# Mixing's weights moved from between the loads of x to behind all of them

## The chip, the cores and the metric

The kernel runs on one core of a Trainium2 chip. The metric is device time in microseconds (us): the time of one execution of the whole program. A kernel's time is the median of its runs; one further execution is taken with the hardware profiler, and every duration below comes from that one.

## The reference, cut to what matters

The input x has 16 images of 64 channels of 128 x 128, in float32. A Hartley layer (a spectral convolution) takes its 20 x 20 lowest modes, mixes the channels of each mode with a weight, transforms back, blurs, and masks. An AFNO block with group norms and a mixture of experts follows.

```python
def dht_2d(x):
    return fftn(x, axes=(2, 3)).real - fftn(flip(x, axis=(2, 3)), axes=(2, 3)).imag
def _neg_k(a):
    return roll(flip(a, axis=(-2, -1)), shift=(1, 1), axis=(-2, -1))
def compl_mul2d(x1, x2):                       # x2: w1, (64, 64, 20, 20)
    x1n, x2n = _neg_k(x1), _neg_k(x2)
    e = lambda a, b: einsum('bixy,ioxy->boxy', a, b)
    return 0.5 * (e(x1, x2) - e(x1n, x2n) + e(x1, x2n) + e(x1n, x2))
x_ht = dht_2d(x)
out_ht[:, :, :20, :20] = compl_mul2d(x_ht[:, :, :20, :20], w1)
y = dht_2d(out_ht) / (H * W)
y = gaussian_smoothing_4d(y)                   # blur over batch, channels, rows, columns
return y * mask                                # |fftfreq(W)| <= 0.25
# then: group norm, AFNO on 32 x 32 modes, residual, group norm, and per image
# a 1x1 feature layer, 2 shared experts, a gate, the best 4 of 16 experts, residual
```

What matters for the change is `_neg_k`: each mode k is mixed with w[k] and also with w[-k], the weight of the mode with both indices negated modulo 20. So a tile with w[k] in its lower half and w[-k] in its upper half is wanted, and the second is w with its inner axis reversed.

## The kernel before

The work runs in a chain of stages: the first ones lie in the first 470 us or so, and the last, the loop over images, takes the rest.

**The x loop** (from L240 on). For each image b of 16 the channels go in eight groups of eight. Each group is one load `xt` of 512 KB on SP's queue (L245, ten buffers, so that SP runs up to ten tiles ahead), 16 matmuls with `fwd1` (L250, the transform along one axis), and one ScalarE copy to `t1` (L253). After the second group of an image comes `along_columns` (L205 to L237) for the image before: 80 matmuls with `fwd2` (L212), a ScalarE copy `pn` (L215), six VectorE additions into `xm` (L219 to L222), and the blur over the batch: VectorE adds `xm`, times a factor, into `x2` for up to nine images (L231, L233). When an image of `x2` has its last term, ScalarE makes its second half (L236, L237). TensorE, ScalarE and VectorE each go through this in the program's order; a DMA is issued when the instructions before it on its queue's engine are through and the waits of its own are met.

**The weights of mixing** sit in `wk` [128, 11, 20, 64]: for k1 = 0 to 10 the lower 64 partitions hold w[k1] as it is in memory, the upper 64 hold w[-k1] with its second index reversed, too. DRAM has them by k1 in pieces of 320 KB. Before the change, at the end of image b (b = 0 to 10) SP issues two loads: the lower half straight to `wk` (L264), the upper half to one staging tile `wn` (L265). At the end of the next image ScalarE copies `wn` to the upper half of `wk`, the first row as it is (L261, 64x64) and the other 19 in reverse order (L262, 64x1216).

**Constants.** Behind the x loop SP issues, by the helper at L172, the loads `blurc`, `dev`, `mean`, `gn1`, `ident`, `sel`, `w1`, `vec`, `spec` (3.2 MB on 100 partitions) and `exw`. Their memory is on the right side, which the x loop used till then, so the first of them waits for the x loop's end.

**Mixing** (L283 on). For k1 = 0 to 10: 20 matmuls, weights from `wk`, data from `x2` (L294), into `psm` (two buffers); then evacuations into `om`, two on ScalarE and one on VectorE beside them or in turn (ScalarE L298, L301, L302; VectorE L299, L303).

**What follows**: the blur over channels (L312; evacuated into `ot` by ScalarE L319 and VectorE L321), the first group norm's statistics (matmuls L397 with `mean`, L406 with `dev`, squares on ScalarE L408, and VectorE's small work L429 to L471), then the AFNO stage per image (L548 with `spec`), and the loop over images (from L826's experts to the store). SP loads the tables of the later stages, `v2` first, between mixing and the statistics; ScalarE copies `v2` to `v2a` and `v2b` (L509 to L514) in two groups of six.

Of the kernel before, what the change touches and what calls it, by code (L numbers as in the profile page):

```python
# [19 lines left out]
K = 20  # L20
# [139 lines left out]
def hartley_afno_moe_kernel(ctx: ExitStack, tc: tile.TileContext, a: dict, out: bass.AP):  # L160
# [6 lines left out]
    def load(pool, name, shape, eng=None):  # L167
        t = pool.tile(shape, F32, name=name + "_sb", tag=name)
        src = a[name]
        if len(shape) == 3 and len(src.shape) == 2:  # L170
            src = src.rearrange("p (a b) -> p a b", b=shape[2])
        (eng or nc.sync).dma_start(t, src)  # L172
        return t
# [13 lines left out]
    with tc.tile_pool(name="modes", bufs=1) as mp:  # L187

        x2 = mp.tile([P, 2, NB, NM], F32, name="x2")
        wk = mp.tile([P, K // 2 + 1, K, C], F32, name="wk")
        gb = blur_matrix(NB)
        with tc.tile_pool(name="f_x", bufs=10) as xp, tc.tile_pool(name="f_t", bufs=2) as tp, \
                tc.tile_pool(name="f_c", bufs=1) as fc, \
                tc.tile_pool(name="f_p1", bufs=4, space=PSUM) as pp1, \
                tc.tile_pool(name="f_p2", bufs=2, space=PSUM) as pp2:
            fwd1 = load(fc, "fwd1", [P, W1], nc.gpsimd)
            fwd2 = None

            wn = fc.tile([P, K, C], F32, name="wn")
            seen = set()

            def along_columns(b, t1):


                ps = pp2.tile([P, K // 2, W1], F32, name="ps2")
                for m in range(K // 2):
                    for t in range(2):
                        for h in range(2):  # L210
                            j = 2 * (2 * m + h) + t
                            nc.tensor.matmul(ps[h * C:(h + 1) * C, m, :], lhsT=t1[:, j, :],  # L212
                                             rhs=fwd2[:, j, :], start=(t == 0), stop=(t == 1))
                pn = tp.tile([P, K // 2, K], F32, name="pn")
                nc.scalar.copy(pn, ps[:, :, K:2 * K])  # L215
                xm = tp.tile([P, K, K], F32, name="xm")
                for half, op in ((0, ALU.add), (1, ALU.subtract)):
                    to = xm[half * C:(half + 1) * C]
                    nc.vector.tensor_tensor(to[:, 0:1], ps[0:C, 0:1, 0:K], pn[0:C, 0:1], op)  # L219
                    nc.vector.tensor_tensor(to[:, 2:K:2], ps[0:C, 1:, 0:K],  # L220
                                            pn[0:C, K // 2 - 1:0:-1], op)
                    nc.vector.tensor_tensor(to[:, 1:K:2], ps[C:P, :, 0:K],  # L222
                                            pn[C:P, ::-1], op)
                xf = xm.rearrange("p a b -> p (a b)")
                for bo in range(NB):
                    g = float(gb[bo, b])
                    if g == 0.0:
                        continue
                    to = x2[:, 0, bo, :]
                    if bo in seen:  # L230
                        nc.vector.scalar_tensor_tensor(to, xf, g, to, ALU.mult, ALU.add)  # L231
                    else:
                        nc.vector.tensor_scalar(to, xf, g, None, ALU.mult)  # L233
                        seen.add(bo)
                    if not gb[bo, b + 1:].any():
                        nc.scalar.mul(x2[0:C, 1, bo], x2[C:P, 0, bo], -1.0)  # L236
                        nc.scalar.copy(x2[C:P, 1, bo], x2[0:C, 0, bo])  # L237

            behind = None
            for b in range(NB):  # L240

                t1 = tp.tile([P, 2 * K, C], F32, name="t1")
                for c0 in range(0, C, 8):
                    xt = xp.tile([P, 8, N], F32, name="xt")
                    nc.sync.dma_start(xt, a["x"][b, :, c0:c0 + 8])  # L245
                    ps = pp1.tile([P, 8, W1], F32, name="ps1")
                    for i in range(8):
                        for h in range(2):
                            cols = slice(h * 64, (h + 1) * 64)
                            nc.tensor.matmul(ps[cols, i, :], lhsT=xt[:, i, cols],  # L250
                                             rhs=fwd1, start=True, stop=True)
                    src = ps[:, :, 0:2 * K].rearrange("p c j -> p j c")
                    nc.scalar.copy(t1[:, :, c0:c0 + 8], src)  # L253
                    if c0 == 8 and behind:
                        along_columns(*behind)
                behind = (b, t1)
                fwd2 = fwd2 or load(fc, "fwd2", [P, 2 * K, W1])

                if 0 < b <= K // 2 + 1:
                    k = b - 1  # L260
                    nc.scalar.copy(wk[C:P, k, 0], wn[C:P, 0])  # L261
                    nc.scalar.copy(wk[C:P, k, 1:K], wn[C:P, K - 1:0:-1])  # L262
                if b <= K // 2:
                    nc.sync.dma_start(wk[0:C, b], a["w"][b])  # L264
                    nc.sync.dma_start(wn[C:P], a["w"][(-b) % K])  # L265
            along_columns(*behind)

        sc = on_modes.enter_context(tc.tile_pool(name="s_c", bufs=1, side="right"))
        blurc = load(sc, "blurc", [P, C])
        dev = load(sc, "dev", [CH, 4, NM])  # L270
        mean = load(sc, "mean", [CH, 4, C])
        gn1 = load(sc, "gn1", [P, 2, C])
        ident = load(sc, "ident", [P, C])
        sel = load(sc, "sel", [CH, 5, 32])
        w1 = load(sc, "w1", [P, 2, P])
        vec = load(const, "vec", [P, V_N])
        spec = load(sc, "spec", [CH, 4, 2 * MD * MD])
        exw = load(sc, "exw", [P, C, NE])

        with tc.tile_pool(name="m_o", bufs=1) as op, \  # L280
                tc.tile_pool(name="m_p", bufs=2, space=PSUM) as pp, \
                tc.tile_pool(name="m_p2", bufs=4, space=PSUM) as pp2:


            om = [op.tile([P, NB, NM // 2], F32, name=f"om{h}") for h in range(2)]
            lok, upk = (t[h * C:(h + 1) * C].rearrange("o b (k2 k1) -> o k1 k2 b", k1=K)
                        for h, t in enumerate(om))
            for k1 in range(K // 2 + 1):

                ps = pp.tile([P, K // 2, 2, NB, 2], F32, name="psm")  # L290
                for m in range(K // 2):
                    k = k1 * K + 2 * m
                    for h in range(2):
                        nc.tensor.matmul(ps[h * C:(h + 1) * C, m].rearrange("p a b q -> p (a b q)"),  # L294
                                         lhsT=wk[:, k1, 2 * m + h, :], rhs=x2[:, :, :, k:k + 2],
                                         start=True, stop=True)
                lo, up = ps[0:C, :, :, :, 0], ps[C:P, :, :, :, 1]
                nc.scalar.copy(lok[:, k1], lo[:, :, 0])  # L298
                nc.vector.tensor_copy(upk[:, k1], up[:, :, 0])  # L299
                if k1 % (K // 2):  # L300
                    nc.scalar.copy(lok[:, K - k1, 0:1], lo[:, 0:1, 1])  # L301
                    nc.scalar.copy(lok[:, K - k1, K // 2 - 1:0:-1], lo[:, 1:, 1])  # L302
                    nc.vector.tensor_copy(upk[:, K - k1, ::-1], up[:, :, 1])  # L303


            for b0 in range(0, NB, 8):
                for cc in range(2):
                    pq = [pp2.tile([CH, 8, C], F32, name="pst") for h in range(2)]
                    for i in range(8):
                        for h, (m0, m1) in ((0, (0, C)), (1, (C, CH)), (1, (0, C)), (0, (C, CH))):  # L310
                            g = slice(h * C, (h + 1) * C)
                            nc.tensor.matmul(pq[h][m0:m1, i, :],  # L312
                                             lhsT=om[h][g, b0 + i, cc * CH + m0:cc * CH + m1],
                                             rhs=blurc[g], start=True, stop=True)
                    for h in range(2):
                        dst = ot[:, 2 * h + cc, b0 * C:(b0 + 8) * C]
                        src = pq[h].rearrange("p b c -> p (b c)")
                        if h:
                            nc.scalar.copy(dst, src)  # L319
                        else:  # L320
                            nc.vector.tensor_copy(dst, src)  # L321


    s3 = ctx.enter_context(ExitStack())
# [635 lines left out]
```

## Time and profile before

| | |
|---|---|
| median of 3 runs | 1856.39 us |
| lowest and highest run | 1854.67 and 1856.52 us |
| the profiled execution: its time | 1848.89 us |
| the profiled execution: its span | 1846.9 us |
| mean granted TensorE clock | 0.976 |
| PE (TensorE matmul) busy | 1701.5 us, 92% |
| ACT (ScalarE) busy | 1378.3 us, 75% |
| DVE (VectorE) busy | 1270.7 us, 69% |
| POOL (GpSimd) busy | 120.9 us, 7% |
| DMA | 181.00 MB, 98 GB/s over the span |

PE, ACT, DVE, POOL and SP are the engines (SP only issues DMAs); PEld is TensorE's weight load, which runs beside the matmuls. L294 is line 294 of the kernel. The profile page cuts the span into 40 slices of 46.2 us and prints the busy share of each engine in tenths, for PEclk the TensorE clock that was granted. A row of windows has, for a stretch of time, the busy time and count of each engine's instructions, the granted clock, the share of the 16 DMA engines that was in use, and GB/s. A row of waits has the engine's instruction, what released it, the idle time, the number of times and the longest. "issue" stands for idle time in which the engine waited for nothing that the profile shows. A row of the timeline has the start, the duration, the engine, the line, what is written and read, and in brackets the idle time ahead and what ended it.

### The profile page before, as it was taken

The numbers are of one execution on the slowest core, as the hardware profiler recorded it, in microseconds if no ns is written. First come the engines' busy times: TensorE is split into PE (matmuls) and PEld (weight loads), VectorE is DVE, ScalarE is ACT, GpSimd is POOL, SyncE is SP. The second block draws the span as 40 slices with busy tenths as digits, with TensorE's granted clock in tenths as the row PEclk, the third lists the DMA queues.
The fourth block names the chain that finished last, engine by engine and source line by source line (L and its number), as shares of the span: only waits on it lengthen the run. The fifth ranks groups of instructions, "written<-read, shape, count | busy, mean of one in ns | idle before, by whom it ended". The sixth has DMA issues, their size and how long they took to land. (4 is left out here: it accounts for less than half of the span.)

```text
span 1846.9 us, 55817 instructions
## 1 busy us (share of the span) xinstructions
PE 1701.5 (92%) x24644; PEld 940.8 (51%) x24644; DVE 1270.7 (69%) x1774; ACT 1378.3 (75%) x1690; POOL 120.9 (7%) x140
## 2 busy tenths in 40 slices
PE   6777769999899999999999999999999999999996
PEld 6776765333645455454545555454545455554521
DVE  1233432322249788797979797797979797887988
ACT  2343343112488998989898999989898999989897
POOL 0000002003010101010110101010100101010110
PEclk8899988999999999999999999999999999999998
DMA  9999841115212222222332222322232322222023
GB/s 337 319 322 326 285 145 48 69 52 145 47 25 70 48 81 57 84 36 82 57 72 58 59 82 36 99 41 81 37 86 53 71 72 46 72 57 71 27 72 92
DMA packets 136129, 181.00 MB, mean 98 GB/s; under 512 B 94201, under 2 KB 95414, under 8 KB 135658
## 3 DMA queue, kind: packets, MB, share of 16 engines
q1 hardware_dynamic: 132192, 171.73, 33.1%
q0 software_dynamic: 3696, 5.71, 1.2%
q8 instruction: 193, 3.16, 0.7%
q14 instruction: 48, 0.39, 0.1%
HBM read 98.29 MB, written 79.11 MB: 96 GB/s over the span
## 5 line engine op out<-in xcount | busy, mean ns | idle before, releaser
L834 DVE SCALAR_TENSOR_TENSOR h<-g,wt,h 128x1024 f32<-128x1024 f32 x512 | 620.9, 1275 | 85.2 <-ACT g L831 85.2
L831 ACT ACTIVATE g<-pe,wl 128x1024 f32<-128x1024 f32 x512 | 539.4, 1131 | 8.9 <-PE pe L826 8.2
L826 PE MATMUL pe<-f,wl 64*64 64x512 f32 x4096 | 494.7, 600 | 1.3 <-issue 0.4
L834 DVE SCALAR_TENSOR_TENSOR h<-g,h 128x1024 f32<-128x1024 f32 x256 | 301.6, 1220 | 56.1 <-ACT g L831 56.1
L831 ACT ACTIVATE g<-pe,vec_sb 128x1024 f32<-128x1024 f32 x256 | 278.7, 1135 | 20.6 <-PE pe L826 20.4
L669 PEld LDWEIGHTS pe<-inv_sb,u 107*128 107x128 f32 x2048 | 234.4, 192 | 64.9 <-ACT g L831 33.2
L826 PEld LDWEIGHTS pe<-f,wl 64*64 64x64 f32 x4096 | 135.6, 132 | 237.3 <-ACT g L831 98.6
L826 PE MATMUL pe<-f,shw 64*64 64x512 f32 x2048 | 252.9, 604 | 0.0
L669 PE MATMUL pe<-inv_sb,u 107*128 107x128 f32 x2048 | 248.8, 279 | 3.2 <-ACT g L831 1.9
L677 ACT ACTIVATE h<-pe,gs 128x1024 f32<-128x1024 f32 x128 | 142.6, 1115 | 73.2 <-PE pe L669 57.3
L250 PE MATMUL ps<-fwd_sb,xt 128*64 128x64 f32 x4096 | 141.5, 232 | 51.0 <-issue 43.1
L681 DVE BATCH_NORM_STATS2 stats<-h 128x6 f32<-128x512 f32 x256 | 160.1, 679 | 25.9 <-ACT h L677 25.8
L250 PEld LDWEIGHTS ps<-fwd_sb,xt 128*64 128x64 f32 x4096 | 135.9, 147 | 54.7 <-issue 46.6
L647 PE MATMUL pe<-inv_sb,bm 64*64 64x128 f32 (+1 forms) x4096 | 144.8, 275 | 1.2 <-issue 1.2
L736 ACT ACTIVATE f<-pe,fb 128x1024 f32<-128x1024 f32 x128 | 144.3, 1137 | 2.2 <-PE pe L732 2.2
L647 PEld LDWEIGHTS pe<-inv_sb,bm 64*64 64x64 f32 (+1 forms) x4096 | 118.5, 124 | 48.1 <-ACT f L736 24.3
L253 ACT COPY t<-ps 128x320 f32<-128x320 f32 x128 | 54.0, 427 | 114.4 <-PE ps L250 114.0
L732 PE MATMUL pe<-h,fs 64*64 64x512 f32 x1024 | 133.9, 611 | 1.6 <-DVE n L709 1.6
L652 ACT COPY u<-pe 105x1024 f32<-105x1024 f32 x128 | 127.4, 1043 | 3.9 <-PE pe L647 2.9
L219 DVE TENSOR_TENSOR xm<-ps,pn 64x20 f32<-64x20 f32 x32 | 5.5, 171 | 172.5 <-ACT pn L215 172.2
L548 PE MATMUL psx<-spec_sb,ot 100*64 100x512 f32 x512 | 115.6, 594 | 0.0
L806 POOL DMA_INDIRECT wl<-exd,ati x64 | 66.9, 1045 | 697.4 <-ACT g L831 605.4
(164 smaller groups left out, 1163.5 us busy)
## 6 DMA issues: line engine op xcount, KB each, us to landing
xt<-in_x_dram SPq DMA_DIRECT2D x128, 512.0 KB
out_dram<-h SPq DMA_DIRECT2D x256, 256.0 KB
o1d<-o SPq DMA_DIRECT2D x16, 512.0 KB
s<-o1d SPq DMA_DIRECT2D x16, 512.0 KB
bm<-od SPq DMA_DIRECT2D x96, 50.0 KB
wk<-in_w_dram SPq DMA_DIRECT2D x11, 320.0 KB
wn<-in_w_dram SPq DMA_DIRECT2D x11, 320.0 KB
spec_sb<-in_spec_dram SPq DMA_DIRECT2D x1, 3200.0 KB
```

The source lines that it names most:

```text
L250: nc.tensor.matmul(ps[cols, i, :], lhsT=xt[:, i, cols], rhs=fwd1, start=True, stop=True)
L548: nc.tensor.matmul(ps[ri * C:(ri + 1) * C], lhsT=ot[:, kc, b * C:(b + 1) * C], rhs=spec[:, kc, ri * 1024 + n * 512:ri * 1024 + (n + 1) * 512],
L647: nc.tensor.matmul(ps[cs, h, i, :], lhsT=bm[rs, 4 * q + i, cs], rhs=inv1[rs, part], start=True, stop=True)
L652: nc.scalar.copy(dst.rearrange("p h s n -> p n h s"), ps[0:KC].rearrange("p h s n -> p n h s"))
L669: nc.tensor.matmul(ps[:, r // 4, r % 4 * N:(r % 4 + 1) * N], lhsT=u[0:KU, 2 * row:2 * row + 2, :].rearrange("p h c -> p (h c)"), rhs=inv2, ...
L677: nc.scalar.activation(h, ps, AF.Identity, bias=gs1[:, 1, box["b"]:box["b"] + 1])
L681: nc.vector.bn_stats(box["stats"][:, 2 * t + p, :], h[:, p])
L732: nc.tensor.matmul(ps[p * C:(p + 1) * C, half], lhsT=box["fs"][rows_], rhs=box["h"][t][rows_, p], start=True, stop=True)
L736: nc.scalar.activation(f, ps, AF.Gelu, bias=box["fb"], accum_out=box["sums"][:, t:t + 1])
L826: nc.tensor.matmul(ps[half * C:(half + 1) * C, p], lhsT=w[rows_], rhs=f[rows_, half], start=True, stop=True)
L831: nc.scalar.activation(g, ps, AF.Gelu, bias=bias)
L834: nc.vector.scalar_tensor_tensor(h, g, share(), h, ALU.mult, ALU.add)
```

## The change

All loads and copies of mixing's weights leave the loop over images. The eleven lower halves are loaded behind the last x tile, ahead of the last `along_columns` in the program's order. The eleven upper halves are loaded inside the block of mixing, into a pool of four staging tiles, and are turned into place by GpSimd for even k and by ScalarE for odd k. The constants from `blurc` to `vec` are loaded after them in SP's queue. `spec` and `exw` get a pool of their own, opened behind the block of mixing and the blur over channels, so that they lie on memory which that block used.

```diff
@@ x loop
-            wn = fc.tile([P, K, C], F32, name="wn")
...
-                if 0 < b <= K // 2 + 1:
-                    k = b - 1
-                    nc.scalar.copy(wk[C:P, k, 0], wn[C:P, 0])
-                    nc.scalar.copy(wk[C:P, k, 1:K], wn[C:P, K - 1:0:-1])
-                if b <= K // 2:
-                    nc.sync.dma_start(wk[0:C, b], a["w"][b])
-                    nc.sync.dma_start(wn[C:P], a["w"][(-b) % K])
+            for k in range(K // 2 + 1):
+                nc.sync.dma_start(wk[0:C, k], a["w"][k])
             along_columns(*behind)
 
-        sc = on_modes.enter_context(tc.tile_pool(name="s_c", bufs=1, side="right"))
-        blurc = load(sc, "blurc", [P, C])
...
-        vec = load(const, "vec", [P, V_N])
-        spec = load(sc, "spec", [CH, 4, 2 * MD * MD])
-        exw = load(sc, "exw", [P, C, NE])
-
-        with tc.tile_pool(name="m_o", bufs=1) as op, \
+        with tc.tile_pool(name="m_o", bufs=1) as op, tc.tile_pool(name="m_w", bufs=4) as wp, \
                 tc.tile_pool(name="m_p", bufs=2, space=PSUM) as pp, \
                 tc.tile_pool(name="m_p2", bufs=4, space=PSUM) as pp2:
+
+            for k in range(K // 2 + 1):
+                wn = wp.tile([P, K, C], F32, name="wn")
+                nc.sync.dma_start(wn[C:P], a["w"][(-k) % K])
+                copy = nc.scalar.copy if k % 2 else nc.gpsimd.tensor_copy
+                copy(wk[C:P, k, 0], wn[C:P, 0])
+                copy(wk[C:P, k, 1:K], wn[C:P, K - 1:0:-1])
+            sc = on_modes.enter_context(tc.tile_pool(name="s_c", bufs=1, side="right"))
+            blurc = load(sc, "blurc", [P, C])
...
+            vec = load(const, "vec", [P, V_N])
...
+    sc2 = on_modes.enter_context(tc.tile_pool(name="s_c2", bufs=1, side="right"))
+    spec = load(sc2, "spec", [CH, 4, 2 * MD * MD])
+    exw = load(sc2, "exw", [P, C, NE])
```

The other lines keep their text; in the kernel after, those from the x loop to the blur over channels have numbers smaller by two (mixing's matmuls are L292), and those from the first group norm on larger by two.

More of the change, by code (lines that the diff above doesn't have):

```diff
@@ L257, in hartley_afno_moe_kernel @@
                 fwd2 = fwd2 or load(fc, "fwd2", [P, 2 * K, W1])
-                if 0 < b <= K // 2 + 1:
-                    k = b - 1
-                    nc.scalar.copy(wk[C:P, k, 0], wn[C:P, 0])
-                    nc.scalar.copy(wk[C:P, k, 1:K], wn[C:P, K - 1:0:-1])
-                if b <= K // 2:
-                    nc.sync.dma_start(wk[0:C, b], a["w"][b])
-                    nc.sync.dma_start(wn[C:P], a["w"][(-b) % K])
-            along_columns(*behind)
-        sc = on_modes.enter_context(tc.tile_pool(name="s_c", bufs=1, side="right"))
-        blurc = load(sc, "blurc", [P, C])
[L270 to L275, printed above, removed]
-        vec = load(const, "vec", [P, V_N])
-        spec = load(sc, "spec", [CH, 4, 2 * MD * MD])
-        exw = load(sc, "exw", [P, C, NE])
-        with tc.tile_pool(name="m_o", bufs=1) as op, \
+            for k in range(K // 2 + 1):
+                nc.sync.dma_start(wk[0:C, k], a["w"][k])
+            along_columns(*behind)
+        with tc.tile_pool(name="m_o", bufs=1) as op, tc.tile_pool(name="m_w", bufs=4) as wp, \
                 tc.tile_pool(name="m_p", bufs=2, space=PSUM) as pp, \
                 tc.tile_pool(name="m_p2", bufs=4, space=PSUM) as pp2:
+            for k in range(K // 2 + 1):
[6 more added lines that the diff above has]
+            blurc = load(sc, "blurc", [P, C])
+            dev = load(sc, "dev", [CH, 4, NM])
+            mean = load(sc, "mean", [CH, 4, C])
+            gn1 = load(sc, "gn1", [P, 2, C])
+            ident = load(sc, "ident", [P, C])
+            sel = load(sc, "sel", [CH, 5, 32])
+            w1 = load(sc, "w1", [P, 2, P])
+            vec = load(const, "vec", [P, V_N])
             om = [op.tile([P, NB, NM // 2], F32, name=f"om{h}") for h in range(2)]
```

## The prediction

> **What bounds the kernel now.** I read the 40 slices first, then a table of windows over the first 300 us, then who waited for whom, then the timeline round 258 to 308 us.
>
> ```profile
> PE   6777769999899999999999999999999999999996
> PEclk8899988999999999999999999999999999999998
> DMA  9999841115212222222332222322232322222023
> ```
>
> From slice 8 on (370 us) TensorE is at 8 or 9 tenths. In the first six slices, 277 us, it is at 6 or 7 with the DMA engines full. The change touches only this head, so everything behind it moves as one block and what the head gains or loses is the result.
>
> ```profile
> core 0: us, PE busy (x) PEld busy (x) DVE busy (x) ACT busy (x) POOL busy (x), PEclk, DMA share, GB/s
> 24.00:69.00 45.00, 32.63 (x866) 31.31 (x865) 12.30 (x36) 13.97 (x30) 0.00 (x0) 0.84 1.01 327
> 69.00:115.00 46.00, 34.06 (x979) 32.62 (x977) 17.01 (x44) 16.84 (x36) 0.00 (x0) 0.91 0.96 328
> 115.00:169.00 54.00, 39.55 (x1193) 38.19 (x1191) 17.50 (x45) 21.28 (x45) 0.00 (x0) 0.95 0.96 311
> 169.00:236.00 67.00, 51.00 (x1567) 49.57 (x1564) 28.12 (x72) 24.13 (x55) 0.00 (x0) 0.95 0.87 304
> 264.00:286.00 22.00, 15.98 (x363) 15.06 (x359) 8.65 (x21) 8.88 (x31) 0.00 (x0) 0.78 0.65 174
> ```
>
> The third figure of a row counts matmuls. The first three rows load x with the weights of mixing between, the fourth x alone. Matmuls per us: 19.2, 21.3, 22.1, then 23.4. So TensorE runs faster once the weights are in, although the DMA share then falls to 0.87: the last stretch is not held by bandwidth.
>
> ```profile
> PE ps L250 <- issue: 41.8, 21, 4.9
> PE ps L212 <- issue: 8.4, 6, 4.1
> PE ps L212 <- ACT t L253: 5.2, 10, 0.5
> PE ps L250 <- DMA xt<-in_x_dram: 1.1, 2, 0.8
> ```
>
> Between 24 and 250 us TensorE hardly waits for x (1.1 us). It idles 50.2 us for nothing that the profile names ("issue"), over some 5100 matmuls: 9.8 ns for each. I read these as gaps that come with DMA load, since the stretch 240 to 258 us, where the DMA share is 0.03, shows only one (2.2 us, at its start).
>
> ```profile
> 257.98 0.33 SPq L172 DMA_DIRECT2D blurc_sb<-in_blurc_dram  x1
> 260.95 0.37 SPq L172 DMA_DIRECT2D spec_sb<-in_spec_dram  x1
> 261.44 6.25 PE L294 MATMUL psm<-x,wk 128*64 128x64 f32 x120 [8.17 <-ACT x L237]
> 291.15 0.24 ACT L509 COPY v2a<-v_sb 64x64 f32<-64x64 f32 x1 [1.43 <-DMA v_sb<-in_v_dram]
> 306.32 0.60 ACT L408 ACTIVATE sq<-psx 100x512 f32<-100x512 f32 x1 [1.93 <-PE psx L406]
> ```
>
> VectorE's last sum into x2 ends at 257.9; I call this D. ScalarE's copies of x2 release mixing at 261.4. Mixing's last product is done at 289.3 (the v_sb load that waits for it is issued at 289.32); I call this M, now D + 31.4.
>
> **The x loop.** Removed: 22 loads of 320 KB from between the x loads and 11 pairs of ScalarE copies (0.24 + 1.20 us). At the rate of the fourth row, 1567/67 = 23.4 matmuls per us, the 3038 matmuls of the first three rows take 129.9 us instead of 145: **-15.1**. Bounds: if the slow early rows have another cause (the clock is 0.84 there), only the third row gains, 1193/23.4 = 51.0 for 54, -3.0; at the rate of 200 to 236 us (894 in 36 us) it is -22.7. Bandwidth allows it: x and fwd2 are 68.4 MB, at 304/0.87 = 349 GB/s 196 us, and the last x load would still be issued near 221.
>
> **Lower rows, behind x.** 11 loads, 3.6 MB, go out while TensorE works off its last ten x tiles. From 236 us to D the DMA engines are idle now, 22 us; at 250 GB/s (between the rows with 327 and with 174) the loads take 14.4. Hidden, but this tail gets its DMA load: 470 matmuls at 9.8 ns are 4.6 us of gaps against 2.2 seen: **+2.4** (0 to 4).
>
> **Mixing.** The staging tiles lie on memory of the x loop, so the first one's load waits for D, as blurc does now. The nearest row for its landing is v_sb: issued 289.32, used 291.15, 1.8 us; 320 KB at 250 GB/s add 1.3: D + 3.1. GpSimd turns k = 0: its nearest row is the 64x1024 copy of L379, 1.93 us, so 2.3 for 1216 elements and 0.3 for the first row: D + 5.7. Bounds: as its memset of L389 (4.36 us for 5120 elements) 1.0; twice the row, 4.6. One product takes 2.0 us (evacuations of 281.10, 283.48, 285.03). ScalarE's k = 1 copy ends about D + 5.9, products 0 and 1 are evacuated by D + 11.2. From there a pair of products costs 1.44 (ScalarE's copy) + 2.0 (the odd product, which waits for it) + 1.5 (evacuations of L298, L299, L301, L302 in turn) = 4.9; the even product and GpSimd's 2.6 us lie under it, and so do the later loads, which wait for a tile that was turned two pairs before. Copy 9 starts at 11.2 + 3 x 4.9 = 25.9, products 9 and 10 end at D + 31.4. Before, the same D + 31.4 held 5.5 us of "issue" gaps under the spec load; now the DMA is light, and I add 1 us: **+1.0** (-2 to +8).
>
> [...]
>
> **Constants behind the weights.** blurc, dev, mean and the rest come after the eleventh upper tile in SP's queue, which goes out when ScalarE has turned k = 5, about D + 18; 13 us before M, hidden. spec (3.2 MB) shares memory with the staging tiles and waits for the k = 9 copy, D + 27.4 or M - 4. spec and exw together filled 264 to 286 us at 174 GB/s; from M - 4 with 1.8 us until the first bytes they end near M + 20. Their users are later (L548 at 320.9 = M + 31.6; exw feeds a gather after 470 us). But v2 stands behind them in SP's queue, and ScalarE has v2's copies between the first and second square of L408. The first ends at M + 15.1, so ScalarE stands 5 us. TensorE has two psx buffers: the fourth L406 group, at 308.05 now, needs the second square (306.32 now), which moves to M + 22.1, and the fifth needs the third. Counted through: **+4.8** (0 if v2 passes spec, 8 if spec ends 3 us later). Also L312, L397 and the first L406 groups, some 310 matmuls, get the DMA load that mixing loses: 9.8 ns each, 3.0 against 0.3 now: **+2.7** (0 to 4). The other moves (vec, bm and onk memsets, squares) find their users over 4 us later.
>
> **Sum.** -15.1 + 2.4 + 1.0 + 4.8 + 2.7 = -4.2. The profiled execution took 1848.89 us (span 1846.9), 7.5 below the median of the runs, 1856.39; I take the difference over: 1852.2.
>
> **Rivals.**
> - *The weights were not what held the x loop.* For: TensorE scarcely waits for x, and the low clock of the first row (0.84) can belong to the start. Against: the rate rises in each row. The gain is then 3 to 7; against costs of 10.9 that is +4 to +8, 1860 to 1864, slower. It decides from a gain below 7.2.
> - *The v2 wait is covered.* spec issued earlier or faster, or v2 not behind it: -4.2 - 4.8 = -9.0, 1847.4. With the upper x rate too, 1840.
> - *A wash.* Gain 12 instead of 15, costs as counted: 1855.
> - *GpSimd is the bound of mixing.* Its six copies take over 4.9 us each (2.6 counted): at 5.5 M is D + 38, +7 more: 1859; at 8, 1874. For: no row shows a reversed GpSimd copy. Against: L379 is strided as well.
>
> **Chances.** Forecast with a net of -3.7 to -8: 0.32. v2 covered or a larger x gain: 0.15. Wash: 0.29. No gain in the x loop: 0.16. GpSimd: 0.08. About 0.2%, 3.7 us, is what a measurement of this kernel can tell from no change. Faster 0.47, same 0.29, slower 0.24. The range from 1841 (v2 covered and nearly the upper x rate) to 1865 (no gain) leaves out the slowest GpSimd copies and some of the highest gain. The faster cases alone lie in 1841 to 1852.5.
>
> **What would show it.** Right: matmuls per us near 23 from 24 us on; D near 245 (257.9 - 15.1 + 2.4); the first L292 product about 5.7 us after D; the GpSimd copies near 2.3 us; ScalarE waiting some 5 us for v2 after the first square. Wrong: x matmul rates as before; GpSimd copies above 4.9 us; no wait for v2; gaps in mixing as long as before.

## The result, and the profile after

After: 1853.85 us (median of 12 runs); before, in the same measurement, 1855.53 us (12 runs). The ratio is 0.9994, with a 95% interval of 0.9978 to 1.001: no change that can be told from none. The profiled execution of after took 1851.94 us (span 1850.2), 1.9 below its median; that of before lay 6.6 below its own, so the two spans must not be subtracted. The stages have to be compared one by one, and over more than one profile.

The slices of after, of TensorE, its clock and the DMA engines:

```profile
PE   6778758999899999999999999999999999999996
PEclk9999989999999999999999999999999999999998
DMA  9788864114212222212332222322232322222023
```

The clock of the first two slices is 9 tenths where before had 8, and the DMA engines are at 7 or 8 in slices 2 to 4, where before had 9. But TensorE's slice 6 fell from 6 to 5, and the DMA load of slices 6 and 7 rose from 4 and 1 to 6 and 4. The windows of the x loop, cut as before:

```profile
core 0: us, PE busy (x) PEld busy (x) DVE busy (x) ACT busy (x) POOL busy (x), PEclk, DMA share, GB/s
24.00:69.00 45.00, 32.65 (x959) 31.73 (x956) 12.30 (x36) 11.21 (x27) 0.00 (x0) 0.92 0.91 338
69.00:115.00 46.00, 35.91 (x1067) 35.20 (x1068) 17.01 (x44) 13.31 (x32) 0.00 (x0) 0.91 0.81 289
115.00:169.00 54.00, 43.46 (x1340) 42.40 (x1336) 23.33 (x60) 18.75 (x44) 0.00 (x0) 0.95 0.83 294
169.00:236.00 67.00, 47.73 (x1429) 46.72 (x1431) 26.88 (x69) 20.47 (x48) 0.00 (x0) 0.93 0.86 277
```

The first three rows hold 3366 matmuls in 145 us, 23.2 per us: the rate that was forecast (23.4). The fourth row seems to fall from 23.4 to 21.3. But a window cut by the clock on the wall does not hold the same work in both kernels: after is ahead by some 17 us here, and its window already takes in TensorE's last tiles, under the loads of the lower rows, which SP issues from 219.1 us on. Cut by the work instead, in each kernel the 1620 matmuls from the 3381st on, and then the last 380 or so of the x loop (first the two rows of before, then those of after):

```profile
171.70:238.50 66.80, 52.54 (x1619) 51.24 (x1621) 26.34 (x66) 24.70 (x56) 0.00 (x0) 0.95 0.87 306
238.50:253.30 14.80, 11.98 (x385) 11.43 (x380) 4.59 (x12) 4.70 (x11) 0.00 (x0) 1.00 0.14 50
154.70:221.50 66.80, 53.83 (x1622) 52.80 (x1623) 28.12 (x72) 22.86 (x53) 0.00 (x0) 0.92 0.81 289
221.50:247.50 26.00, 15.13 (x383) 14.44 (x377) 4.59 (x12) 4.80 (x11) 0.00 (x0) 0.87 0.76 167
```

Behind the third row nothing was gained or lost until the last 380 matmuls, and these took 26.0 us instead of 14.8. What TensorE waited for in those two stretches, before and after:

```profile
PE ps L250 <- issue: 2.2, 1, 2.2
PE ps L248 <- issue: 10.4, 3, 5.2
```

And between 24 and 250 us in after:

```profile
PE ps L248 <- issue: 32.2, 20, 5.2
PE ps L210 <- issue: 22.8, 8, 4.1
PE ps L210 <- ACT t L251: 0.5, 1, 0.5
```

The unnamed waits did not shrink as a whole: 55.0 us where before had 50.2. Of the ten waits for ScalarE one is left, and the two for x are gone. The timeline behind the x loop, whose last VectorE sum (D) now ends at 252.1:

```profile
252.20 17.86 SPq L267 DMA_DIRECT2D wn<-in_w_dram  x11
256.72 1.19 POOL L270 COPY wk<-wn 64x1216 f32<-64x1216 f32 x1
256.82 0.47 PE L292 MATMUL psm<-x,wk 128*64 128x64 f32 x2 [9.32 <-POOL wk L269]
277.58 0.31 SPq L172 DMA_DIRECT2D spec_sb<-in_spec_dram  x1
281.43 0.33 SPq L172 DMA_DIRECT2D v_sb<-in_v_dram  x1
287.01 2.84 PE L310 MATMUL pst<-blurc_sb,om 64*36 64x64 f32 x128 [3.10 <-issue]
303.82 0.24 ACT L511 COPY v2a<-v_sb 64x64 f32<-64x64 f32 x1 [2.37 <-DMA v_sb<-in_v_dram]
```

One sees the steps of the forecast: the upper tiles are requested at D, GpSimd turns the first, TensorE starts 4.7 us behind D; mixing ends (M) at 281.4; spec is in flight under the blur over channels, where TensorE idles 3.1 us; and v2, requested at 281.4 behind spec, is used 22 us later.

### The profile page after: what moved, and what is told of

Read it like the earlier page. It is cut to its first block, busy times and chain, and to the rows that moved or that the text cites. A ratio compares the mean times of both kernels' runs of the same rounds, so it can differ in the third digit from the quotient of the medians.

```text
span 1850.2 us, 55827 instructions
## 1 busy us (share of the span) xinstructions
PE 1699.1 (92%) x24644; PEld 935.7 (51%) x24644; DVE 1270.3 (69%) x1774; ACT 1369.7 (74%) x1678; POOL 129.1 (7%) x152
## 5 line engine op out<-in xcount | busy, mean ns | idle before, releaser
L248 PE MATMUL ps<-fwd_sb,xt 128*64 128x64 f32 x4096 | 146.9, 235 | 40.0 <-issue 33.8
L248 PEld LDWEIGHTS ps<-fwd_sb,xt 128*64 128x64 f32 x4096 | 140.9, 150 | 43.0 <-issue 36.7
```

The source lines that it names most:

```text
L248: nc.tensor.matmul(ps[cols, i, :], lhsT=xt[:, i, cols], rhs=fwd1, start=True, stop=True)
```

## The experiments

Each is compared with before on the same chip; "D", "M" and the stages are read from its profile.

**before_again and after_again**: the two kernels unchanged, one more profile each.

> The kernel before, profiled once more, to see how far the pieces of the head move from one execution to the next. If the differences seen between the two profiles (end of the x loop, D, 5.8 us earlier; mixing 2.1 us shorter; 3.5 us lost in the blur over channels, 1.4 in the mean, 1.8 in the statistics) are the change's, D comes within 2 us of 257.9, mixing from D to its last product within 2 us of 31.4, and statistics end 60 us after D as before. If D is mostly chance (the late instruction packets fall differently each time), it differs by 4 us or more. The loop over images (1521 us from 321 to the last store) should differ by 1 to 5 us from chance alone.

> The kernel after, profiled once more. If the two profiles' difference is the change's: D within 2 us of 252.1, the last product of mixing within 2 us of 281.4, the first product of the AFNO stage within 2 us of 319.7, and ScalarE waits again for v2 between the first and the second square. If chance: D 4 us or more away. GpSimd's reversed copy of 1216 elements again 1.20 us.

Before had D at 269.2 this time (257.9 in the first profile), after at 253.5 (252.1). So D of before moves by 11 us from one execution to the next, and the first profile was at its lucky end; D of after moved by 1.4 here, and lies between 252.1 and 258.7 in the five profiles that share its x loop. Mixing from D to M took 32.0 (31.3) in before and 30.0 (29.3) in after. TensorE's waits in the x loop of before_again:

```profile
PE ps L250 <- issue: 44.2, 22, 5.4
PE ps L212 <- issue: 5.4, 3, 3.4
PE ps L212 <- ACT t L253: 5.2, 10, 0.5
PE ps L250 <- DMA xt<-in_x_dram: 2.4, 2, 1.4
```

The same kinds as in the first profile and the same 49.6 us of unnamed waits, though the loop was 11 us longer: the rest was the clock, 0.87 between 7 us and the last matmul of the x loop against 0.92, with 195.5 us of busy time against 184.7 for the same 5368 records. In after_again ScalarE waited for v2 as forecast (timeline behind 305 us):

```profile
305.80 0.24 ACT L511 COPY v2a<-v_sb 64x64 f32<-64x64 f32 x1 [4.17 <-DMA v_sb<-in_v_dram]
307.65 1.10 PE L408 MATMUL psx<-ot,dev_sb 100*100 100x512 f32 x2 [2.48 <-ACT sq L410]
309.47 12.06 PE L408 MATMUL psx<-ot,dev_sb 100*100 100x512 f32 x20 [0.72 <-ACT sq L410]
```

TensorE stood 3.2 us in all, and then the last 20 matmuls took 12.06 us where after's first profile had 8.83: a clock of 0.50 was granted from 309.5 to 316. So the wait cost 6.8 us here and 1.8 in the first profile, and the first product of the AFNO stage, expected within 2 us of 319.7, came at 324.9.

Here 3.2 us of waiting in two pieces stood ahead of 6.5 us at a clock of 0.50. Shorter waits stood ahead of the same clock in the x loop of after: behind those of 2.26 and 2.24 us that end at 28.45 and 41.02 us, 0.50 was granted from 28.7 to 32.1 and from 42.3 to 45.7. Not behind every wait: at the end of the one of 2.21 us, 57.11, it was 1.00 and stayed so until 69.6. So a late packet can cost its wait and, at a clock of 0.50, some time more.

**x_ten_tiles**: what the x loop is without its transfers.

```diff
...
-                    xt = xp.tile([P, 8, N], F32, name="xt")
-                    nc.sync.dma_start(xt, a["x"][b, :, c0:c0 + 8])
+                    n = b * 8 + c0 // 8
+                    if n < 10:
+                        xts.append(xp.tile([P, 8, N], F32, name=f"xt{n}"))
+                        nc.sync.dma_start(xts[n], a["x"][b, :, c0:c0 + 8])
+                    xt = xts[n % 10]
```

> After, with only the first ten groups of x loaded and their tiles used over and over (left out: the other 118 loads of x), so the x loop runs with hardly any DMA beside it. If the idle gaps of TensorE (60 us of them behind 24 us, each behind a multiple of 126 matmuls and ending 1.4 us after a 16 KB packet of instructions landed) come from instruction packets that queue behind data, they shrink to under 15 us and D falls from 252 to about 200. If each 16 KB piece has its gap whatever the load (1.45 us for each of 41 pieces), D stays at 240 to 250. If the loop were held by x's arrival, D would fall too, but the gaps that end with an instruction packet would stay.

D came to 184.5, even below the 200 expected. TensorE's waits from 24 to 180 us:

```profile
PE ps L252 <- issue: 4.8, 2, 3.7
PE ps L211 <- ACT t L255: 0.5, 1, 0.5
```

With hardly any data in flight (DMA share 0.02 from 69 us on) 4.8 us of unnamed waits are left of the 55.0 in after, and the clock is 1.00 from 69 us on. So they do come with DMA load, as the prediction read them. In before and after those over 1 us come some 126 matmul rows, or a multiple of that, behind one another and end 1.2 to 1.7 us after a packet of 16 KB of the instruction queue has landed. The trace of before has 193 such packets (that of after 194) for 24,644 matmul and as many weight-load rows, some 128 of each to a packet: the reading that fits all this is that TensorE had used up its instructions, and the next piece was late.

**x_five_buffers**: bufs=5 instead of 10 in the pool of x.

> After, with five buffers for x instead of ten. If the instruction packets queue behind the x loads that SP has issued ahead, a shorter queue makes the gaps shorter: D falls by 5 to 15 us. If the queue of loads is set by the pace at which tiles come free (a load is issued when a tile is free, 3 to 4 are under way at a time either way), the gaps stay near 60 us and D within 3 us of 252. x now lands 10 to 15 us ahead of its use; with five buffers that is some 5 us less, so waits for x could come in: D later by up to 10 us.

D 250.7. The unnamed waits went down to 28.2 us, but waits for x of 22.4 us took their place (1853.12 us, one run); the sum, 50.6 for 55.0, changed little. Five x buffers cost nothing in this one run, which frees 20 KB per partition.

**in_loop_gpsimd**: before, with nc.scalar.copy of the two reversal copies replaced by nc.gpsimd.tensor_copy.

> Before, with the reversal in the x loop done by GpSimd instead of ScalarE; the loads stay between the x loads. If what the x loop gained was the end of ScalarE's weight copies (TensorE waited ten times 0.5 us for ScalarE's t copy before, once after), D comes near 252 to 254 although every load stays, the ten waits go, and the time is 5 to 10 us (0.3 to 0.5%) shorter. If it was the DMA load of the weights, D stays at 258 to 269 and the time within 0.2% of before.

It was slower, 1862.92 us, ratio 1.0044 (1.0028 to 1.006), D 271.7; why is not shown. And the ten waits stayed:

```profile
PE ps L212 <- ACT t L253: 5.2, 10, 0.5
```

So ScalarE's weight copies did not cause them. They go with the order of TensorE's instructions. With the weight loads in the loop the scheduler puts along_columns' 40 matmul instructions (80 rows of the profile) in one piece for 12 of 16 images; without them 14 of 16 images have 7, then an x group, then 33, and the x group covers ScalarE's copy.

**all_gpsimd**: after, all upper tiles turned by GpSimd.

```diff
-                copy = nc.scalar.copy if k % 2 else nc.gpsimd.tensor_copy
+                copy = nc.gpsimd.tensor_copy
```

> After, with all eleven upper tiles turned by GpSimd. If ScalarE's copies set mixing's pace (its pairs of products are 4.3 us apart, of which 1.44 are ScalarE's copy), the pairs come 2.9 us apart and mixing from D to its last product takes 29.3 - 5 x 1.4 = 22 us. If the arrival of the upper tiles sets it (1.6 to 2 us each behind D), mixing stays at 27 us or more. The head is then up to 7 us shorter, as far as the v2 wait does not take it back: time 0 to 7 us below after's (0 to 0.4%).

Mixing took 25.6 us from D to M (29.3 and 30.0 in after): about half of the gain that the copies alone would have given. Ratio to before 0.9988 (0.9975 to 1.0001). What mixing gained, v2 took back:

```profile
ACT v2a L511 <- DMA v_sb<-in_v_dram: 7.3, 1, 7.3
```

**v2_first**: after, with spec and exw requested behind v2.

```diff
-    sc2 = on_modes.enter_context(tc.tile_pool(name="s_c2", bufs=1, side="right"))
-    spec = load(sc2, "spec", [CH, 4, 2 * MD * MD])
-    exw = load(sc2, "exw", [P, C, NE])
...
     v2 = load(kp, "v2", [P, 2, C])
+    sc2 = on_modes.enter_context(tc.tile_pool(name="s_c2", bufs=1, side="right"))
+    spec = load(sc2, "spec", [CH, 4, 2 * MD * MD])
+    exw = load(sc2, "exw", [P, C, NE])
```

> After, with v2 loaded ahead of spec and exw in SP's queue. If the wait of ScalarE for v2 between the first two squares is what lengthened the statistics (19.3 and 24.3 us in two profiles, 17.5 before), they are back at 17.5 and the head is 2 to 7 us shorter; time 0.1 to 0.4% below after's, the like below before's. If spec, now issued some 4 us later, becomes late for the AFNO stage, its first product starts after 319.7. The gaps in the blur over channels stay (3 to 4 us).

```profile
284.12 0.33 SPq L172 DMA_DIRECT2D v_sb<-in_v_dram  x1
284.49 0.37 SPq L172 DMA_DIRECT2D spec_sb<-in_spec_dram  x1
287.98 0.24 ACT L511 COPY v2a<-v_sb 64x64 f32<-64x64 f32 x1
298.70 17.48 PE L408 MATMUL psx<-ot,dev_sb 100*100 100x512 f32 x40
```

v2's copies now lie under the blur over channels, and the 40 matmuls of the statistics are one piece of 17.48 us, as before. spec was in time. Ratio to before 0.9979 (0.9967 to 0.9991). That v2's place in the queue lengthened the statistics is shown by the stage; in the time, the interval overlaps that of after (0.9978 to 1.001).

**gpsimd_v2_first**: both edits.

> After, with both of the mends that helped alone: all eleven upper tiles turned by GpSimd, and v2 loaded ahead of spec. If the two are independent, mixing from D to its last product takes 25.6 us (as with GpSimd alone) and the statistics 17.5 us (as with v2 first alone), so the head is 6 to 10 us shorter than after's and the time 0.3 to 0.5% below before's. If spec, issued behind v2 and so behind the end of mixing, now is late for the AFNO stage, the first product of that stage waits for it and 2 to 4 us come back.

Ratio 0.9983 (0.9969 to 0.9996): not more than v2_first alone. Mixing took 26.6 us and the statistics 17.5, as each edit alone. But D was 257.6 in its profile, and the mean's matmuls (L399) ran at a low clock (0.52), 7.0 us instead of 3.6. The two parts add up in their stages; in the time the sum is not seen.

**tail_v2_first**: the weights turned while the x loop ends. Five x buffers, four staging tiles, and

```diff
             for k in range(K // 2 + 1):
                 nc.sync.dma_start(wk[0:C, k], a["w"][k])
+                wn = wp.tile([P, K, C], F32, name="wn")
+                nc.sync.dma_start(wn[C:P], a["w"][(-k) % K])
+                nc.gpsimd.tensor_copy(wk[C:P, k, 0], wn[C:P, 0])
+                nc.gpsimd.tensor_copy(wk[C:P, k, 1:K], wn[C:P, K - 1:0:-1])
             along_columns(*behind)
```

in place of the loop in the block of mixing; v2 ahead of spec.

> After, with five x buffers, and in the memory of the other five the staging tiles: lower and upper rows are loaded by turns behind the last x tile and turned by GpSimd while the x loop ends; v2 ahead of spec. If mixing's own floor is its evacuations (1.45 us for each product), the first product comes 3.7 us after D as before and the last 16 to 18 later, so M = D + 20 to 22 instead of D + 29.3; with D 250 to 254, M near 273 and the statistics done near 301: 15 us less than after, 0.6 to 0.8% faster than before. Rival: 7.2 MB in the tail lengthens TensorE's gaps there, or the tiles land late: D at 256 or later, or mixing waits for GpSimd, and half of it is lost.

The rival came, by a way not thought of: ratio 1.0017 (0.9999 to 1.0035), mixing's first to last product 37 us (24.6 in after).

```profile
PE psm L290 <- DVE om L295: 9.9, 1, 9.9
PE psm L290 <- ACT x L235: 9.0, 1, 9.0
```

Two products were done, and then TensorE stood 9.9 us for the first evacuation. The pool of staging tiles closed with the x loop, mixing's output `om` was laid on them, and the first copy into it (272.16) came when GpSimd had turned the last tile (272.14).

**tail_kept**: the same with six x buffers and three staging tiles, in a pool that stays open through mixing.

```diff
-    with tc.tile_pool(name="modes", bufs=1) as mp:
+    with tc.tile_pool(name="modes", bufs=1) as mp, tc.tile_pool(name="m_w", bufs=3) as wp:
```

> The version with the weights loaded by turns behind x, but with six x buffers and three staging tiles that stay open through mixing, so that mixing's output does not lie on them (there the first evacuation waited 9.9 us, until the last tile was turned). If that overlap alone cost the 37 us of mixing, the first product still comes 3.7 us after D and the last one about when the last tile is turned, D + 17 to 20: M near 274, 0.4 to 0.6% faster than before. Rival: the tiles land one in 2.75 us, with three of them one in 3 us or more, so the last is turned at 275 or later and M stays near D + 24; gain 0.2 to 0.4%.

1839.88 us, ratio 0.9936 (0.9914 to 0.9957): faster than before, and with no overlap with after's interval (0.9978 to 1.001).

```profile
255.35 6.06 PE L290 MATMUL psm<-x,wk 128*64 128x64 f32 x120 [8.22 <-ACT x L235]
276.58 0.33 SPq L172 DMA_DIRECT2D v_sb<-in_v_dram  x1
```

These timeline rows show mixing started by ScalarE's copy of x2, as before the change, not by a turned tile; M is 276.4 with D at 252.8. That is the rival's D + 24, but not by its way: GpSimd had turned the last tile at 265.4, and the last products wait for evacuations into `om`. The last 380 matmuls of the x loop had 6.4 us of unnamed waits, where after had 10.4. One wait is left to mend, spec's at the AFNO stage (1.9 us of TensorE's waits behind 250 us):

```profile
PE psx L548 <- DMA spec_sb<-in_spec_dram: 1.9, 1, 1.9
```

**before_seven_more**: before, with seven matmuls of the first image done twice.

> Before, with seven of the first matmuls done twice (14 more instructions on TensorE, ahead of the loop over images; left out: nothing). After has 14 semaphore instructions more on TensorE than before, and its time from the first AFNO product to the last store was 1525.8 and 1526.2 us where before had 1521.3 and 1522.6; the 9th and 12th image took 85 and 86 us where before had 84.1 and 83.6. If that comes from where the 16 KB pieces of TensorE's instructions end (the packet of the next piece then stands ahead of a store's last write), it comes here too: 1525 to 1527 us, the same two images long. If it comes from something else of the change, it stays at 1521 to 1523.

The shift was twice the one meant: the profile has 14 matmul rows and 14 weight loads more, 28 instructions, not 14. From the first AFNO product to the last store it took 1530.7 us, against 1521.3 and 1522.6 in before. So a handful of instructions far ahead, 0.5 us of work, came with a loop over images that was 8 to 9 us longer. The images that got longer are partly others: the 3rd, 6th, 8th, 9th, 12th and 14th, by 1.1 to 2.1 us each. In this profile two of ScalarE's waits for a store are 2.3 and 1.9 us long and end 1.6 us behind such a packet, where before's two profiles have none over 1.5 us. This fits packets that stand ahead of a store's write, but accounts for a part of the 8 to 9 us only, in one profile. That after's two long images come from its 14 semaphore instructions is likely, and was not shown by itself.

**after_extra_scalar**: after, and the 22 loads of weights once more in the x loop, from ScalarE's queue.

> After, and at the end of each of the images 0 to 10 the two pieces of weights are loaded once more, into a tile that nothing reads (added: 22 loads of 320 KB, issued from ScalarE's queue so that TensorE's order stays that of after: 80 matmuls of along_columns as 7 and 33 around the next group, in 12 of 16 images, where before has 4). Before had D at 257.9 to 271.7 in four profiles, after 252.1 to 258.7 in five with ten buffers. If the weights' bytes between the x loads are what slowed the x loop, D goes to 262 to 270 and the time is 0.3 to 0.7% above after's. If it was TensorE's order (10 waits of 0.5 us for ScalarE's copy, which go with the order), D stays at 252 to 258 and the time within 0.2% of after's. Both together: D near 260.

```profile
ACT t L252 <- DMA extra<-in_w_dram: 40.8, 10, 9.1
```

Inconclusive. D was 289.3, ratio 1.0223 (1.0202 to 1.0244), but ScalarE stood 40.8 us: each load had to wait for the one before it into the same tile, and the t copies stood behind. So how much of the x loop's gain is the bytes and how much TensorE's order stays open.

## Why the prediction was right or wrong

The forecast was 1852.2, in a range of 1841 to 1865, and the measured 1853.85 lies in it; the change against before was to be -4.2 us and is -1.1 (-4.1 to +1.9 by the interval). The range holds before's own 1855.53, so that lying in it says little, and no change is the outcome of the wash, which had 0.29. Its sum (a gain of 12, costs as counted) is not the one that came. The stages, as means over the profiles of kernels that share them:

| stage | forecast | measured | from |
|---|---|---|---|
| x loop, to its last 380 matmuls | -15.1 | -22.1 | they begin at 238.5, 251.0, 245.2 in before's three profiles; at 221.5, 221.9, 224.8, 221.6, 224.0 in the five with after's x loop |
| the last 380 matmuls, to D | +2.4 | +13.5 | 18.9 to 32.4 |
| both, that is D | -12.7 | -8.6 | before 257.9, 269.2, 264.4 (with seven matmuls more); after 252.1, 253.5, and 258.7, 253.9, 257.6 in the kernels with its x loop |
| mixing, D to M | +1.0 | -1.6 | 31.4 to 29.8 |
| blur and mean | +2.7 | +3.9 | 10.8 to 14.7 |
| statistics | +4.8 | +4.3 | 20.9; after 22.7 and 27.8 |
| AFNO and the loop over images | 0 | +3.5 | 1521.3, 1522.6; after and the three others 1524.6 to 1526.1 |
| sum | -4.2 | +1.5 | |

The sum of single profiles, of which before's D alone spreads over 11 us, agrees with the timed -1.1 within what it can. That the forecast lies near it is partly luck: two terms were better than counted (by 7.0 and 2.6 us) and two worse (by 11.1 and 3.5). Of the signs that were to show it right, the rate near 23 and ScalarE's wait for v2 came; D near 245 did not.

- **The x loop.** Its rate came as forecast, 23.2 matmuls per us in the first three rows, and the gain is larger over all profiles because before's first one was its fastest. The reading behind it was half wrong. That the gaps come with DMA load is right: x_ten_tiles has almost none. That the weights' share of the load sets them is not: from 7 us to the last 380 matmuls they were 49.3, 49.1 and 58.8 us in before's profiles and are 46.3 to 51.2 in the five others, with x's loads alone. What went instead, as means: 9.3 us of busy time (174.7 to 165.4; the clock was 0.92, 0.86 and 0.96, and is 0.94 in all five), some 6 us of waits for ScalarE, of which the prediction had shown 5.2 in a row and costed none, 3.5 us of waits for x and `fwd2`, and 3.3 us of unnamed waits.
- **Lower rows: the term that was mis-sized.** 14.4 us of loads were counted as hidden, with +2.4 for gaps, 9.8 ns for each matmul. The tiles did land in time: 1.6 us apart (205 GB/s), 243.5 the last, 8.6 us ahead of D, though slower than the 250 GB/s of the author's estimate. But under them TensorE's last 380 matmuls cost 13.5 us more, not 2.4: three waits of 2.4, 5.2 and 2.8 us in after (10.4 in all, 10.6 to 11.7 in the four others, 1.2 to 2.2 in before), and a clock of 0.87 (0.75 to 0.87) instead of 1.00. A gap belongs to a packet, not to a matmul: 9.8 ns for each of 126 would be 1.2 us a packet. Why the packets are later under these loads than under x, at a smaller DMA share (0.76 for 0.81 to 0.91), is open.
- **Mixing.** First product at D + 4.7 for 5.7 forecast, pairs 4.3 us apart for 4.9. GpSimd's reversed copy took 1.20 us where 2.3 was taken from L379, so the rival of GpSimd as the bound was far off; the lower bound of 1.0, worked out from the memset of L389, was nearer. L379 reads across its rows (1.93 us for 1024 elements); a reversed run of whole rows (1.20 us for 1216) is not like it.
- **Constants.** The wait of ScalarE for v2 came as told: 5 us forecast, 2.4 and 4.2 seen, and v2_first removes it. The gaps in the blur came too (4.0 us of unnamed waits in after, 3.4 in after_again); in after a low clock followed in the mean (0.71 from 292 to 297 us), in after_again it did not.
- **The rest of the kernel.** "Everything behind it moves as one block" failed. The loop over images became 3.5 us longer, in the 9th and 12th image above all, in all five profiles of the kernels with after's x loop. In the 12th, ScalarE waits for a store:

```profile
1496.72 1.11 ACT L679 ACTIVATE h<-pe,gs 128x1024 f32<-128x1024 f32 x1 [2.36 <-DMA out_dram<-h]
```

In the packets of after, a 16 KB instruction packet runs from 1494.56 to 1495.44, and the store's last 4-byte write ends at 1495.45, right behind it; in after_again the same (1499.59 and 1499.60). In before the write ended at 1493.37, while that packet had just begun (1493.31 to 1494.19).

## What to carry to other kernels

Before a load is moved for bandwidth's sake, ask which wait it would end, and what runs where it goes: here x's own transfers kept the unnamed waits nearly as long as ever (3.3 us less, of some 50), and under the moved loads the last ones were longer (10.4 us in the last 380 matmuls, 2.2 before). Compare stretches of the same work, not of the same time: a window at the same place made one row look slower that was not. A load that is moved behind another in a queue moves everything behind it in that queue (ScalarE waited 2.4 and 4.2 us for v2 behind spec, and not in v2_first), and a staging pool should not lie where the next stage writes (9.9 us in tail_v2_first) or where the last one still works: with both mended (tail_kept, which also turns all tiles on GpSimd) the idea is worth 0.6%. Take a second profile before a stage's length is used in a sum.

## What the runs showed of the hardware that was not expected

The DMA queue of the instructions (q8 on the profile page) has 193 packets in before and 194 in after, all of 16 KB. In a loop of short matmuls (some 126 rows to a packet, 4 us of work) under x's transfers (DMA share 0.8 to 1.0) TensorE stood 50.2 us (before) and 55.0 us (after) between 24 and 250 us in unnamed waits, and each of these over 1 us ended 1.2 to 1.7 us after such a packet had landed. With x's transfers left out (x_ten_tiles) there were 4.8 us of them.

Such a packet can also stand ahead of a store's last write, as in after's 12th image (1495.44 and 1495.45). How much such packets move a long loop is open: 28 instructions more, far ahead of it, came with 8 to 9 us more in its 1522, in one profile.
